# Gathering q during the second expert layer, k during the third and v during the attention, with six result buffers

## The chip, the cores and the metric

The kernel runs on one core of one Trainium2 chip. A core has five engines that each run an instruction stream of their own: PE (matmuls), DVE and ACT (element-wise work, copies out of PSUM), POOL (here mostly index-driven transfers) and SP (here only plain transfers). PEld is PE's loading of weights, shown as an engine of its own. Transfers from any of them are carried out by 16 DMA engines. The metric is the time on the device, in microseconds (us): the median of three runs. Beside the runs stands one profiled execution, from which all views below are taken.

## The reference

For 16 sequences of 256 tokens with 256 features, `x` first goes through a causal cross-attention with 16 heads, whose keys and values come from a context of the same size, and the result is added to `x`. After a layer norm, three "fast feedforward" layers (ffn q, k and v) follow. Each sends a token down a binary tree of depth 4 to one of 16 experts and applies only that expert's two small matrices:

```
leaf   = tree(x, node_w, node_b)                 # one of 16, per token
hidden = relu(x @ w1[leaf] + b1[leaf])           # 256 -> 64
out    = hidden @ w2[leaf] + b2[leaf]            # 64 -> 256
```

With q, k, v from the three layers, the last step is a plain attention within each sequence, over 256 features at once: `x + softmax(q k^T / 16) v`.

## The kernel before

The kernel has three stages. The **first** (lines 154 to 674) computes the cross-attention in groups of two sequences, the layer norm, the routing of every token, and a sort by expert: for each ffn, POOL scatters the normalised rows (`xnb`, 128 rows of 1 KB in a transfer) into DRAM arrays `xs`, so that the tokens of an expert lie together. Some scatters of ffn 1 and 2 are left over and are sent by `send_one` during the second stage.

The **second** (`second_stage`, line 723) runs the experts. For each of the three ffns there are NJ = 47 tiles of 128 sorted tokens, 141 steps in all, written out by hand: the order of PE, DVE and POOL is the order of the program. In step `i`:

- SP fetches the rows of tile i+6 (`fetch`, L758, 128 KB into one of ten `xt` buffers; the address is read from a table in SBUF by a register load, L755).
- DVE copies the expert's first matrix to a fixed place (`staged`, L775, one of four `ws1`), PE turns the tile (`turn`, L784), ACT copies it out.
- PE does the first matmul of tile i-2 (`layer1`, L795), and ACT applies bias and relu into one of four `hT` (L797).
- PE does the second matmul of tile i-3 (`layer2`, L805). For every pair of tiles DVE copies the result into one of three buffers `y` (L811), and SP writes it to the DRAM array `ys` (L813, 256 KB). A buffer can be used again when that write has landed.
- In steps 47, 51 and 55 DVE also works out, for one ffn each, where in `ys` every token's row stands (`spots`, L743 to L747).

To go back to the order of the tokens, POOL gathers 128 rows of `ys` at a time (L857, one transfer of 128 KB). Each of q, k and v needs 32 gathers, and each can start only when all of its `ys` has been written. POOL is kept in step with the rest by a tiny copy, `tick` (L831), that reads the newest `hT` before each of its transfers; `hT` in turn cannot be overwritten before its tick has read it. The line that says in which steps POOL sends something, and the orders in which the generators of `gathers` hand out the transfers, are these:

```python
if i % 2 == 0 and (4 <= i < 40 or f == 1 and j >= 12) or f == 2 and j >= 4 and i % 4 != 3:
```

```python
if f == 1:
    order = [(0, t) for t in range(EARLY)]                                                # EARLY = 16
elif f == 2:
    order = [(g, t) for t in range(ROOM) for g in (1, 0) if g or t >= EARLY]              # ROOM = 24
```

So during ffn 0 the left-over scatters are sent; during ffn 1, 16 gathers of q in every second step; during ffn 2, 24 gathers of k and 8 more of q, in three of four steps. Each goes into a buffer of its own (24 for q, 24 for k).

The **third** stage (`third_stage`, line 863) is the attention, in 32 query tiles. Here only PE's order is written by hand, the other engines' order comes from a scheduler. POOL has to do the remaining 48 gathers: all 32 of v, into six buffers that come free with the results, and the last eight of q and of k, into buffers that come free when PE has turned the first sequences. In the built program POOL's first gathers of the stage are two of q and two of k, then v 0 to 5, then eight more of q and k, and so on. For a query tile PE turns q and k (L879), multiplies them (L887), turns the probabilities (L902) and multiplies them with v (L911); DVE and ACT do the softmax between, and SP writes the tile out (L914).

Of the kernel before, what the change touches and what calls it, by code (L numbers as in the profile page):

```python
# [30 lines left out]
FP = mybir.dt.float32  # L31
# [6 lines left out]
P = 128  # L38
NB, S, D = 16, 256, 256
# [5 lines left out]
NF, NL, NN, HW = 3, 16, 15, 64  # L45
PB = 2
TP = PB * S
NP = NB // PB
# [9 lines left out]
def xattn_ffn(ctx: ExitStack, tc: tile.TileContext, x, ctxT, wq, wk, wv, wo,  # L58
              node_w, node_b, w1, b1, w2, b2, out):
    nc = tc.nc  # L60
    PS = bass.MemoryType.PSUM
    ET = mybir.EngineType
# [6 lines left out]
    ys = [nc.dram_tensor(f"ys_{f}", (NJ * P, D), FP, kind="Internal").ap() for f in range(NF)]  # L69
# [14 lines left out]
    for e in range(2):  # L84
        for dst, n, row in ((own, DH, DH * e), (first, 1, DH * (1 - e))):
            t = const.tile([P, 1], FP, tag=f"rows{e}{n}", name=f"rows{e}{n}")
# [67 lines left out]
    def first_stage(stack):  # L154
# [514 lines left out]
        def finish():  # L669
            send(len(rows))  # L670
            ending[0] = False
            return scatters, lambda: send(1)

        return finish

# [47 lines left out]
    def second_stage(stack, scatters, send_one, rest):  # L723
        one = stack.enter_context(tc.tile_pool(name="f_one", bufs=1, **AFTER))
        three = stack.enter_context(tc.tile_pool(name="f_three", bufs=3, **AFTER))
        ten = stack.enter_context(tc.tile_pool(name="f_ten", bufs=10, **AFTER))
        ps = stack.enter_context(tc.tile_pool(name="ps_f", bufs=2, space=PS, **AFTER))
        leaf_weights(2, one, nc.sync)
# [71 lines left out]
        def layer2(i):  # L800
            f, j = work[i]
            if j % 2 == 0:
                ys_ps[f, j // 2] = ps.tile([P, 2, D], FP, tag="y", name=f"py_{f}_{j}")
            py = ys_ps[f, j // 2]
            nc.tensor.matmul(py[:, j % 2, :], hT[i % NBUF],  # L805
                             w2_sb[f][:, bass.ds(leaf_of.pop(i), 1), :].rearrange("h l d -> h (l d)"),
                             start=True, stop=True)
            if j % 2 or j == NJ - 1:
                n = j % 2 + 1
                y = three.tile([P, 2, D], FP, tag="y", name=f"y_{f}_{j}")  # L810
                nc.vector.tensor_copy(y[:, 0:n], py[:, 0:n])  # L811
                j0 = j - j % 2
                nc.sync.dma_start(out=ys[f][j0 * P:(j + 1) * P, :].rearrange("(t p) d -> p t d", p=P), in_=y[:, 0:n])  # L813

        fetched = {i: fetch(i) for i in range(6)}
        for i in range(len(work) + 4):
            if i + 6 < len(work):
                fetched[i + 6] = fetch(i + 6)
            if i in (NJ, NJ + 4, NJ + 8):
                spots((i - NJ) // 4)  # L820
            if i < len(work):
                staged(i)
                turn(i, fetched.pop(i))
            if 0 <= i - 2 < len(work):
                layer1(i - 2)
            if 0 <= i - 3 < len(work):
                layer2(i - 3)
            f, j = divmod(i, NJ)
            if i % 2 == 0 and (4 <= i < 40 or f == 1 and j >= 12) or f == 2 and j >= 4 and i % 4 != 3:

                nc.gpsimd.tensor_copy(tick, hT[(i - 2) % NBUF][0:1, 0:1])  # L831
                if f == 0:
                    send_one()
                else:
                    next(rest[f], None)
        assert next(rest[1], rest) is rest and next(rest[2], rest) is rest


    ROOM, EARLY = 24, 16

    def gathers(pool, f):


        if f == 1:
            order = [(0, t) for t in range(EARLY)]
        elif f == 2:
            order = [(g, t) for t in range(ROOM) for g in (1, 0) if g or t >= EARLY]
        else:
            order = []
        for b in range(NB if f == NF else 0):  # L850
            order += [(2, 2 * b), (2, 2 * b + 1)]
            if 3 <= b < 3 + (2 * NB - ROOM) // 2:
                t = ROOM + 2 * (b - 3)
                order += [(g, t + i) for g in range(2) for i in range(2)]
        for f, t in order:
            g = pool.tile([P, D], FP, tag=f"g{f}", bufs=6 if f == 2 else ROOM, name=f"g_{f}_{t}")
            nc.gpsimd.indirect_dma_start(  # L857
                out=g, out_offset=None, in_=ys[f],
                in_offset=bass.IndirectOffsetOnAxis(ap=spot_of[0][:, f, t:t + 1], axis=0))
            got[f, t] = g  # L860
            yield

    def third_stage(stack, rest):
        two = stack.enter_context(tc.tile_pool(name="a_two", bufs=2, **AFTER))
        three = stack.enter_context(tc.tile_pool(name="a_three", bufs=3, **AFTER))
        ps = stack.enter_context(tc.tile_pool(name="ps_a", bufs=2, space=PS, **AFTER))

        def wanted(f, t):
            while (f, t) not in got:
                next(rest)  # L870
            return got.pop((f, t))

        def turn(b, f):

            pt = ps.tile([P, DC, S], FP, tag="t", name=f"pt_{f}_{b}")
            for i in range(2):
                g = wanted(f, 2 * b + i)
                for c in range(DC):
                    nc.tensor.transpose(pt[:, c, i * P:(i + 1) * P], g[:, c * P:(c + 1) * P], ident)  # L879
            tT = two.tile([P, DC, S], FP, tag=f"T{f}", name=f"T_{f}_{b}")  # L880
            (nc.scalar.copy if f else nc.vector.tensor_copy)(tT, pt)
            return tT

        def probs(b, qt, qT, kT):
            pz = ps.tile([P, S], FP, tag="z", name=f"pz_{b}_{qt}")
            for d in range(DC):
                nc.tensor.matmul(pz, qT[:, d, qt * P:(qt + 1) * P], kT[:, d, :],  # L887
                                 start=(d == 0), stop=(d == DC - 1))
            mx = three.tile([P, 1], FP, tag="fmx", name=f"fmx_{b}_{qt}")
            nc.vector.tensor_reduce(mx, pz, AX.X, ALU.max)  # L890
            nc.vector.tensor_scalar(mx, mx, -D ** -0.5, None, ALU.mult)
            pr = three.tile([P, S], FP, tag="pr", name=f"pr_{b}_{qt}")
            den = three.tile([P, 1], FP, tag="den", name=f"den_{b}_{qt}")
            nc.scalar.activation(pr, pz, AF.Exp, bias=mx, scale=D ** -0.5, accum_out=den)
            rd = three.tile([P, 1], FP, tag="frd", name=f"frd_{b}_{qt}")
            nc.vector.reciprocal(rd, den)
            return pr, rd

        def turned(b, qt, pr):
            pt = ps.tile([P, 2, P], FP, tag="u", name=f"ptf_{b}_{qt}")  # L900
            for kt in range(2):
                nc.tensor.transpose(pt[:, kt, :], pr[:, kt * P:(kt + 1) * P], ident)  # L902
            pT = two.tile([P, 2, P], FP, tag="fpT", name=f"fpT_{b}_{qt}")
            nc.scalar.copy(pT, pt)
            return pT

        def result(b, qt, pT, rd, v):
            t = 2 * b + qt
            po = ps.tile([P, D], FP, tag="o", name=f"po3_{t}")
            for kt in range(2):  # L910
                nc.tensor.matmul(po, pT[:, kt, :], v[kt], start=(kt == 0), stop=(kt == 1))  # L911
            ot = three.tile([P, D], FP, tag="ot", name=f"ot_{t}")
            nc.vector.scalar_tensor_tensor(ot, po, rd, xres[:, t, :], ALU.mult, ALU.add)
            nc.sync.dma_start(out=out[t * P:(t + 1) * P, :], in_=ot)  # L914

        n = 2 * NB
        made, pTs, turns, vs = {}, {}, {0: (turn(0, 0), turn(0, 1))}, {}
        for i in range(n + 2):
            b, qt = divmod(i, 2)
            if i < n:  # L920
                made[i] = probs(b, qt, *turns[b])
                if b + 1 < NB:
                    turns.setdefault(b + 1, []).append(turn(b + 1, qt))
            if 0 < i <= n:
                pTs[i - 1] = turned(*divmod(i - 1, 2), made[i - 1][0])
            if i > 1:
                b, qt = divmod(i - 2, 2)
                if qt == 0:
                    vs[b] = [wanted(2, 2 * b + kt) for kt in range(2)]
                result(b, qt, pTs.pop(i - 2), made.pop(i - 2)[1], vs[b])  # L930

    spot_of, got = [], {}
    with ExitStack() as stack:
        with tc.manual_schedule(engines={ET.PE, ET.DVE, ET.Activation, ET.Pool}):
            finish = first_stage(stack)
        scatters, send_one = finish()
    pool = ctx.enter_context(tc.tile_pool(name="gather", bufs=2, **AFTER))
    rest = [gathers(pool, f) for f in range(NF + 1)]
    with ExitStack() as stack:
        with tc.manual_schedule(engines={ET.PE, ET.DVE, ET.Pool}):  # L940
            second_stage(stack, scatters, send_one, rest)
    with tc.manual_schedule(engines={ET.PE}):
        third_stage(ctx, rest[NF])


# [33 lines left out]
```

## Time and profile before

| | |
|---|---|
| median of the runs | 721.13 us (721.12 to 721.37) |
| the profiled execution's own time | 746.15 us |
| its span, first to last instruction | 744.2 us |
| mean granted PE clock | 0.929 |
| busy, share of the span: PE, PEld, DVE, ACT, POOL | 83%, 62%, 56%, 48%, 48% |
| first `ph` matmul of the second stage | at 446.5 us |
| first turned q of the third stage | at 640.1 us |
| gathers of `ys` rows (L857) | 96, 963 ns of POOL each |
| stores of `ys` (L813) and loads of `xt` (L758) | 72 and 141 |

The profiled execution is 25 us longer than the runs. Times in the views count from the start of the span. In a list of instructions the columns are start, duration, engine, line, operation, output<-input, count, and in brackets how long the engine was idle before and what ended it; "issue" means that the profile shows nothing it waited for. A wait is put down to the release that came last.

### The profile page before, as it was taken

The page shows a single profiled execution, that of the slowest core. Times are in us where ns is not written, and L with a number is a line of the kernel's source. Part 1 is how long each engine was busy: PE and PEld are TensorE (multiplying, and loading weights), DVE is VectorE, ACT ScalarE, POOL GpSimd, SP SyncE. Part 2 cuts the span into 40 slices and gives each one's busy share as a digit, 9 for nine tenths or more (in the row PEclk, how much of TensorE's full clock was granted, in tenths as well). Part 3 has the DMA queues.
Part 4 walks back from the last instruction along what each step waited for, and adds up shares of the span by engine and source line. Part 5 has one row for each costly group of instructions (what it writes and reads, how often), then busy time and mean ns, then how long its engine had stood idle before and what let it go on. Part 6 is the DMA issues. An engine that isn't in the chain of part 4 may idle for free.

```text
span 744.2 us, 17407 instructions
## 1 busy us (share of the span) xinstructions
PE 619.8 (83%) x5453; PEld 458.7 (62%) x5453; DVE 417.7 (56%) x1924; ACT 353.8 (48%) x920; POOL 357.9 (48%) x530
## 2 busy tenths in 40 slices
PE   4579999999898999989874529998998788847998
PEld 2346666666565655656553318777986667636886
DVE  0157777868677786876864253445543243414564
ACT  5457666665665556455332105543554344313443
POOL 7133554267576566665674413410341565664331
PEclk9779999999999999999987558998999899969999
DMA  9303942002011110111112316876787787433333
GB/s 263 106 17 101 324 129 61 1 24 80 30 59 48 37 61 30 37 51 44 44 43 93 92 43 210 256 229 207 233 261 219 232 258 226 148 104 93 114 114 93
DMA packets 65388, 89.59 MB, mean 120 GB/s; under 512 B 7921, under 2 KB 54289, under 8 KB 65297
## 3 DMA queue, kind: packets, MB, share of 16 engines
q1 hardware_dynamic: 53186, 52.77, 23.2%
q0 software_dynamic: 12112, 35.71, 16.0%
q8 instruction: 45, 0.74, 0.4%
q14 instruction: 45, 0.37, 0.2%
HBM read 46.90 MB, written 41.55 MB: 119 GB/s over the span
## 4 chain that ended last, share of the span: by engine, by line
PE 61%; DVE 11%; POOL 7%; issue 7%; ACT 6%; DMA 5%; SPq 1%; another core or an unknown queue 1%; DVEq 0%; POOLq 0%; ACTq 0%
PE ph L795 8%; PE py L805 7%; PE bank L275 6%; PE bank L452 6%; PE bank L472 6%; PE pz L887 4%; PE po L911 4%; PE px L784 4%; PE bank L427 4%; PE bank L304 3%; DMA ys<-y 3%; PE bank L295 3%; DVE junk L434 2%; PE pt L879 2%; POOL xs L407 2%
## 5 line engine op out<-in xcount | busy, mean ns | idle before, releaser
L434 DVE CUSTOM_DVE_ANT_0 junk<-bank,later 128x128 bf16<-128x128 f32 (+1 forms) x512 | 147.7, 352 | 24.4 <-PE bank L427 22.1
L462 POOL TENSOR_SCALAR_AFFINE_SELECT pT<-pT 128x1024 f32<-128x1024 f32 x64 | 70.3, 1098 | 137.7 <-ACT pT L457 128.9
L457 ACT ACTIVATE pT<-bank 128x384 f32<-128x384 f32 x256 | 104.6, 493 | 67.1 <-PE bank L452 40.8
L857 POOL DMA_INDIRECT g<-ys,spot_i x96 | 92.5, 963 | 72.0 <-PE po L911 31.9
L407 POOL DMA_INDIRECT xs<-xnb,dest_i x96 | 95.9, 999 | 28.4 <-issue 20.1
L795 PE MATMUL ph<-xT,ws 128*128 128x128 f32 x564 | 91.6, 287 | 12.8 <-DVE ws L775 10.0
L811 DVE COPY y<-py 128x512 f32<-128x512 f32 x72 | 48.9, 680 | 85.7 <-DMA ys<-y 29.3
L805 PE MATMUL py<-w,hT 65*128 x282 | 88.8, 397 | 7.8 <-ACT hT L797 5.8
L797 ACT ACTIVATE hT<-ph,b_sb 64x128 f32<-64x128 f32 x141 | 51.1, 362 | 81.9 <-PE ph L795 48.7
L795 PEld LDWEIGHTS ph<-xT,ws 128*128 128x128 f32 x564 | 77.5, 199 | 17.9 <-issue 9.7
L452 PE MATMUL bank<-xqT,xkT 32*128 32x256 f32 (+1 forms) x1024 | 71.5, 356 | 12.4 <-DVE xqT L443 4.4
L452 PEld LDWEIGHTS bank<-xqT,xkT 32*128 32x128 f32 x1024 | 57.7, 192 | 34.2 <-DVE xqT L443 14.9
L472 PE MATMUL bank<-pT,va 128*32 128x256 f32 (+1 forms) x1024 | 57.5, 343 | 17.8 <-DVE mx L434 9.3
L427 PE MATMUL bank<-xkT,xqT 32*128 32x128 f32 (+1 forms) x1024 | 63.9, 361 | 0.0
L784 PE MATMUL px<-ident,xt 128*128 128x128 f32 x282 | 57.0, 284 | 4.8 <-DMA xt<-xs 4.2
L788 ACT COPY xT<-px 128x512 f32<-128x512 f32 (+1 forms) x71 | 41.3, 582 | 39.0 <-PE px L784 34.6
L831 POOL COPY tick<-hT 1x1 f32<-1x1 f32 x67 | 12.0, 179 | 96.1 <-ACT hT L797 95.4
L784 PEld LDWEIGHTS px<-ident,xt 128*128 128x128 f32 x282 | 40.2, 147 | 23.8 <-DMA xt<-xs 5.8
L472 PEld LDWEIGHTS bank<-pT,va 128*32 128x32 f32 x1024 | 29.8, 112 | 37.7 <-issue 19.1
L222 ACT ACTIVATE junkq<-xres,negm 128x256 bf16<-128x256 f32 x64 | 31.8, 502 | 43.4 <-DVE negm L217 33.4
L775 DVE COPY ws<-w 128x128 f32 x141 | 33.7, 240 | 31.0 <-DVE ws L775 14.5
L805 PEld LDWEIGHTS py<-w,hT 65*128 65x128 f32 x282 | 44.5, 198 | 10.0 <-ACT hT L797 7.1
(166 smaller groups left out, 1038.0 us busy)
## 6 DMA issues: line engine op xcount, KB each, us to landing
xt<-xs SPq DMA_DIRECT2D x141, 128.0 KB
ys<-y SPq DMA_DIRECT2D x69, 256.0 KB
xs<-zero POOLq DMA_DIRECT2D x3, 2048.0 KB
xres<-in_x SPq DMA_DIRECT2D x8, 512.0 KB
ctx<-in_ctxT SPq DMA_DIRECT2D x8, 512.0 KB
w<-in_w POOLq DMA_DIRECT2D x4, 1024.0 KB
out<-ot SPq DMA_DIRECT2D x32, 128.0 KB
w<-in_w SPq DMA_DIRECT2D x2, 1024.0 KB
```

The lines of the kernel that those rows point to most:

```text
L407: s = nc.gpsimd.indirect_dma_start(out=xs[f], out_offset=bass.IndirectOffsetOnAxis(ap=dest_i[:, t, f:f + 1], axis=0), in_=row, in_offset=None)
L427: nc.tensor.matmul(bk[g][:, qt * P:(2 * qt + 1) * P], q[r, qt * P:(qt + 1) * P], k[r, 0:(qt + 1) * P], start=True, stop=True)
L434: nc.vector.tensor_tensor_reduce(junk[:, 0:n], bk[g][:, qt * P:qt * P + n], later[:, S - n:], -1.0, -MASKED, ALU.add, ALU.min, mxs[c % 2][ ...
L452: nc.tensor.matmul(bk[g][:, 0:3 * P].rearrange("p (k n) -> p k n", n=P)[:, kt:3 - kt:2 - kt, :], k[r, kt * P:(kt + 1) * P], q[r, kt * P:], ...
L457: nc.scalar.activation(pf[:, g, :], bk[g][:, 0:3 * P], AF.Exp)
L462: nc.gpsimd.affine_select(out=pf[:, :, 0:S], in_=pf[:, :, 0:S], compare_op=ALU.is_ge, fill=0.0, base=0, pattern=[[0, G], [0, 2], [1, P]], ...
L472: nc.tensor.matmul(av[r, kt * P:], vas[p % 2][:, 2 * b + kt, 8 * (c // 2) + 2 * g + c % 2, :], pT[:, g, kt:3 - kt:2 - kt, :], start=(kt == ...
L784: nc.tensor.transpose(pt[:, i % 2, c, :], xt[:, c * P:(c + 1) * P], ident)
L795: nc.tensor.matmul(ph, w[:, c, :], xTs[i // 2][:, i % 2, c, :], start=(c == 0), stop=(c == DC - 1))
L797: nc.scalar.activation(hT[i % NBUF][0:HW], ph[0:HW], AF.Relu, bias=b1_sb[:, f].rearrange("h c e -> h (c e)")[:, bass.ds(leaf(i, ET.Activat ...
L805: nc.tensor.matmul(py[:, j % 2, :], hT[i % NBUF], w2_sb[f][:, bass.ds(leaf_of.pop(i), 1), :].rearrange("h l d -> h (l d)"), start=True, st ...
L857: nc.gpsimd.indirect_dma_start(out=g, out_offset=None, in_=ys[f], in_offset=bass.IndirectOffsetOnAxis(ap=spot_of[0][:, f, t:t + 1], axis=0))
```

## The change

Four things are edited.

1. The gathers of q are all put into ffn 1 and those of k all into ffn 2: 32 each, in the steps with tile number j from 7 on, except where j is a multiple of five. (8 of 40 steps are left out.) The scatters during ffn 0 stay where they were. One generator hands out all 64.
2. For the 32 gathers of one kind there is now less need of buffers of their own, because tiles that are no longer read take the rest: the first-layer weights `w1_sb[0]` (eight places) for q, and `w1_sb[1]` (eight) with the last two normalised tiles `xnb` (four each) for k. q has 24 buffers and k 16.
3. In the third stage POOL gathers only v, in an order that is now written by hand too: two before the first query tile, then one a query tile, two ahead, into six buffers as before.
4. The result buffers `y` are six instead of three.

```diff
@@ first_stage, finish @@
-            return scatters, lambda: send(1)
+            return scatters, lambda: send(1), [xns["b", p] for p in range(NP - 2, NP)]
@@ second_stage @@
+        six = stack.enter_context(tc.tile_pool(name="f_six", bufs=6, **AFTER))
...
-                y = three.tile([P, 2, D], FP, tag="y", name=f"y_{f}_{j}")
+                y = six.tile([P, 2, D], FP, tag="y", name=f"y_{f}_{j}")
...
-            if i % 2 == 0 and (4 <= i < 40 or f == 1 and j >= 12) or f == 2 and j >= 4 and i % 4 != 3:
+            if f == 0 and i % 2 == 0 and 4 <= i < 40 or 0 < f < NF and j >= 7 and j % 5:
                 nc.gpsimd.tensor_copy(tick, hT[(i - 2) % NBUF][0:1, 0:1])
                 if f == 0:
                     send_one()
                 else:
-                    next(rest[f], None)
+                    next(rest, None)
@@ gathers @@
-    def gathers(pool, f):
...
+    def gathers(pool, sent):
+        for f in range(2):
+            old = [w1_sb[f].rearrange("p c (t d) -> p (c t) d", d=D)] + (sent if f else [])
+            old = [t[:, i] for t in old for i in range(t.shape[1])]
+            room = 2 * NB - len(old)
+            for t in range(2 * NB):
+                got[f, t] = gather(pool.tile([P, D], FP, tag=f"g{f}", bufs=room, name=f"g_{f}_{t}") if t < room
+                                   else old[t - room], f, t)
+                yield
+
+    def gather(g, f, t):
+        nc.gpsimd.indirect_dma_start(
+            out=g, out_offset=None, in_=ys[f],
+            in_offset=bass.IndirectOffsetOnAxis(ap=spot_of[0][:, f, t:t + 1], axis=0))
+        return g
@@ third_stage @@
-        def wanted(f, t):
-            while (f, t) not in got:
-                next(rest)
-            return got.pop((f, t))
+        def v(t):
+            if t < n:
+                got[2, t] = gather(pool.tile([P, D], FP, tag="g2", bufs=6, name=f"g_2_{t}"), 2, t)
...
+        for t in range(2):
+            v(t)
...
         for i in range(n + 2):
             b, qt = divmod(i, 2)
+            v(i + 2)
@@ at the end @@
-    with tc.manual_schedule(engines={ET.PE}):
-        third_stage(ctx, rest[NF])
+    with tc.manual_schedule(engines={ET.PE, ET.Pool}):
+        third_stage(ctx, pool)
```

More of the change, by code (lines that the diff above doesn't have):

```diff
@@ L834, in second_stage, with third_stage @@
                 else:
-                    next(rest[f], None)
-        assert next(rest[1], rest) is rest and next(rest[2], rest) is rest
-    ROOM, EARLY = 24, 16
-    def gathers(pool, f):
[L844 to L863, printed above, removed]
+                    next(rest, None)
+        assert next(rest, rest) is rest
+    def gathers(pool, sent):
[12 more added lines that the diff above has]
+        return g
+    def third_stage(stack, pool):
         two = stack.enter_context(tc.tile_pool(name="a_two", bufs=2, **AFTER))
@@ L876, in turn @@
             for i in range(2):
-                g = wanted(f, 2 * b + i)
+                g = got.pop((f, 2 * b + i))
                 for c in range(DC):
@@ L928, in third_stage @@
                 if qt == 0:
-                    vs[b] = [wanted(2, 2 * b + kt) for kt in range(2)]
+                    vs[b] = [got.pop((2, 2 * b + kt)) for kt in range(2)]
                 result(b, qt, pTs.pop(i - 2), made.pop(i - 2)[1], vs[b])
@@ L935, in xattn_ffn @@
             finish = first_stage(stack)
-        scatters, send_one = finish()
+        scatters, send_one, sent = finish()
     pool = ctx.enter_context(tc.tile_pool(name="gather", bufs=2, **AFTER))
-    rest = [gathers(pool, f) for f in range(NF + 1)]
+    rest = gathers(pool, sent)
     with ExitStack() as stack:
```

## The prediction

> **What bounds the kernel now.** I read the shares by engine first (PE busy 83% of 744.2 us, DMA uneven), then the busy time by stretch, which cuts the span into the stages that the edit touches. Columns: stretch, its length, busy us (instructions) of PE, PEld, DVE, ACT, POOL, then granted clock, DMA share, GB/s.
>
> ```profile
> 446.00:503.60 57.60, 54.00 (x358) 46.46 (x358) 22.99 (x63) 28.72 (x68) 19.02 (x34) 0.96 0.75 229
> 503.60:565.80 62.20, 56.49 (x378) 49.56 (x377) 29.70 (x81) 30.16 (x72) 18.75 (x33) 0.95 0.79 233
> 565.80:640.00 74.20, 62.23 (x391) 51.48 (x390) 28.77 (x76) 30.53 (x74) 37.01 (x64) 0.95 0.76 227
> 640.00:681.30 41.30, 23.40 (x113) 18.76 (x111) 11.44 (x36) 8.99 (x28) 25.24 (x27) 0.81 0.39 116
> 681.30:744.20 62.90, 59.32 (x338) 51.95 (x337) 35.30 (x110) 27.00 (x84) 20.20 (x22) 0.99 0.35 103
> ```
>
> The first three rows are the three ffns, q, k and v, 47 tiles each. In PE's timeline a tile takes 1.10 us when nothing is late, so 47 need 51.7 us. The ffns therefore lose 57.6 - 51.7 = 5.9, 62.2 - 51.7 = 10.5 and 74.2 - 51.7 = 22.5 us. The last two rows are the attention stage: from 681.3 on a query tile takes 2.385 us (25 tiles to 740.9, then the tail); in the 41.3 us before only 7 were finished, which at that pace need 16.7. The loss there is 24.6 us, with DMA at 0.39 and PE busy 57%. So 63 us of the span are stalls in exactly these stages. Before 446 us the edit changes nothing but one load (below).
>
> Next, the waits in the three ffns (us in total, times, longest), and the chain of waits at the start of the attention stage (start, us, what).
>
> ```profile
> DVE y L811 <- DMA ys<-y: 29.3, 26, 2.9
> ...
> PE ph L795 <- DVE ws L775: 10.0, 11, 3.0
> ```
>
> ```profile
> 646.97 2.52 DMA g<-ys,spot_i
> ...
> 652.83 11.14 issue
> 663.98 2.08 PE pz L887 x4
> ```
>
> DVE waits 29.3 us for a result buffer `y` whose write has not landed; the expert weights `ws` are copied on the same in-order engine, so PE waits behind. One such delay grows: PE's timeline at the border of ffns 0 and 1 (start, us, engine, line, what, count, idle before it):
>
> ```profile
> 505.97 0.38 PE L784 MATMUL px<-ident,xt 128*128 128x128 f32 x2
> 509.33 1.19 PE L795 MATMUL ph<-xT,ws 128*128 128x128 f32 x4 [2.97 <-DVE ws L775]
> ...
> 515.43 0.47 PE L784 MATMUL px<-ident,xt 128*128 128x128 f32 x2
> 516.62 0.38 PE L784 MATMUL px<-ident,xt 128*128 128x128 f32 x2
> ```
>
> DVE came late to the row positions (1.6 us of `own`, `spot`, `spot_i`), PE stood still, and its matmuls then took twice their time (1.06 against 0.61 us for a group) until 515.4: four tiles in 10.65 us instead of 4.4, 6.25 us for one late DVE. Last, POOL's timeline at ffn 2:
>
> ```profile
> 573.04 0.17 POOL L831 COPY tick<-hT 1x1 f32<-1x1 f32 x1 [7.88 <-ACT hT L797]
> 579.35 0.97 POOL L857 DMA_INDIRECT g<-ys,spot_i  x1 [6.13 <-DMA xt<-xs]
> 580.32 0.21 POOL L831 COPY tick<-hT 1x1 f32<-1x1 f32 x1
> 580.70 0.98 POOL L857 DMA_INDIRECT g<-ys,spot_i  x1 [0.16 <-issue]
> 581.68 0.18 POOL L831 COPY tick<-hT 1x1 f32<-1x1 f32 x1
> 582.02 0.98 POOL L857 DMA_INDIRECT g<-ys,spot_i  x1 [0.16 <-issue]
> ```
>
> The first k gather stood 6.13 us for the last k rows to be written, then six went out back to back, 1.33 us apiece. Just there, at 582 to 589, ACT, DVE and SP all hang (waits of 3.3 and 5.0 us whose releaser is unknown; SP's small instructions each start 0.7 us late), PE takes 12.75 us for five tiles (582.26 to 595.01), 7.3 over its pace, 2.1 of them at half clock. The 11.14 us at 652.8 has the same companion: 16 gathers in a row, 1.25 us apart, while ACT stands from 649.9 to 663.3.
>
> **Part by part.**
>
> Six `y` buffers. A buffer now comes round after six pairs (13.2 us) instead of three (6.6); the chain of waits has steps of 2.4 to 3.8 us on such a write, so I let the 29.3 us of DVE waits go. What PE loses to them, tile by tile over 1.10 us: 5.3 us in ffn 0, about 3 before 565, 3.2 at 567 to 580, and the 6.25 at the border if DVE now arrives early (the last position group, at 518, cost PE nothing). What is late next: SP. It issues two loads and one store per pair; undisturbed 2.31 us, with its hitches about 2.5, so 1.25 us a tile against PE's 1.10, and its lead shrank from 5.7 to 3.2 us between tiles 10 and 26. I give ffn 0 only 3 of its 5.3 us back (ends: 0 and 5.3).
>
> q gathers: 32 instead of 16 in ffn 1, from tile 7 and in four of five tiles, not from 12 in every second. Each issues a tick (0.18), a gather (0.98) and gaps, 1.33 us of POOL; four of them take 5.3 of the 5.5 us of five tiles, so POOL runs nearly back to back. Behind POOL stand only more gathers and ACT: `hT` cannot be overwritten before its tick has read it, four tiles later, which a POOL up to 4.4 us late does not reach. Cost of a gather to PE: 0 by ffn 1 (row below, one every second tile, PE busy 20.83 of 21.0 us at 261 GB/s); 0.41 us by ffn 2 after 593.7 (three of four tiles; 30 tiles in 42.1 us, 9.1 over their pace, beside 22 gathers); 1.2 us by the burst (7.3 us over six). The pattern is nearest to steady ffn 2: 0.41 x 32 = 13.2 us; ends 0 and 39.
>
> ```profile
> 530.00:551.00 21.00, 20.83 (x151) 18.59 (x150) 9.20 (x26) 11.88 (x29) 10.62 (x19) 1.00 0.90 261
> ```
>
> Against ffn 1's present loss of 10.5, which goes with the `y` waits: +2.7.
>
> k gathers: 32 in ffn 2 as before, but from tile 7 instead of 4. The last k store leaves three tiles earlier relative to that, so neither the 6.13 us wait nor the burst should come: -7.3 us; the `y` waits there go (-3.2); 32 gathers cost 13.2 instead of 9.1 over 22 (+4.1). Sum -6.4 (ends -19.6, all gathers free, and +19, all at the burst's price).
>
> One rule of the Trainium skill speaks against this. "DMA: Bandwidth & Descriptors", section "Issuing engines are not separate DMA queues", says that transfers started from SP, ScalarE or GpSimd share the same 16 DMA engines and interleave, so a gather moved from the attention stage (share 0.35 to 0.39) to an ffn (0.75 to 0.79) takes its room from `xt` and `ys`. Per tile ffn 1 would ask 131 + 131 + 0.8 x 131 = 367 KB; in 1.10 us that is 333 GB/s, more than any 10 us of this trace moved (268 at share 0.90, so some 295 when full). By the rule, 16 x 131 KB = 2.1 MB at 265 GB/s lengthen the ffns by 7.9 us. By the row above, 16 gathers cost nothing; by ffn 2's row (245 GB/s, gaps left) something other than bytes decided. I take the 13.2 above, which is more than the rule asks; with the rule's 7.9 in its place the sum below would be 5.3 us lower.
>
> Attention stage: 32 gathers instead of 48, v first and two ahead. The q and k gathers that stood before v (640.7 to 645.7) go, but v's must wait for the last `ys` write, landing near 643.4, and the first result needs two of them: the 2.5 us wait stays. The run of 16 shrinks to six. If the hang goes with the run, 11.1 us, the slow clock after it (2) and a second stop at 676 to 679 (4) go: -16; if the hang has another cause, about 0. Later v gathers wait for a freed buffer as before.
>
> At nothing: gathers into `w1_sb` 0 and 1 and two `xn` tiles, whose last readers end over 20 us before in ffns 0 and 1; ACT's and DVE's order in the attention stage is unchanged in the built kernel. The larger pool moves addresses, so ffn 2's w1 load now waits for the last normalising (about 426 us, was 402); with w2's, 2 MB at 250 GB/s end near 435, ahead of the first `xt` at 441.8. Without that cover it would be up to 8 us.
>
> **Sum.** -3 + 2.7 - 6.4 - 16 = -22.7 us of the profiled 746.15. The runs shown have a median of 721.13, 25 us less: part of what the profiled execution loses is not there, and hangs of sequencers are the likeliest part. So I count the two hang terms at half (8 of 16, and 3.65 of 7.3): -3 + 2.7 - 2.75 - 8 = -11, giving 710 us.
>
> **Rivals.** (a) Slower: back-to-back gathers hang the sequencers wherever they stand, now through ffn 1 too. With p us lost per gather the change is 64p + 3 (ffn 0's rest) - 38.9 (what the ffns lose now) - 12 (attention, between its ends), zero at p = 0.75. The burst's 1.2 speaks for it, the 0.41 of steady ffn 2 and 0 in ffn 1 against. At p = 1 it is +16: 737 us. (b) SP and the 16 engines set the ffns: the `y` wait becomes a wait for `xt`, the ffns gain 3 and pay 7.9, attention gains 8: 718 us. For it: SP's 1.25 us a tile, the rule; against: 1.10 us a tile for 20 us at share 0.90. (c) The hang is no matter of gathers and stays: only the ffn terms, -3: 718 us.
>
> **How the numbers follow.** Forecast (700 to 715) 0.5; (c) 0.12; (b) 0.14; (a) 0.2; a better end, both hang terms whole and gathers free, 0.04. Range 694 to 727: (a)'s upper part is left out. A difference of 0.2%, 1.4 us, is about what a measurement can tell from no change. Faster 0.71 (the forecast, the better end, most of (b) and (c)), same 0.06, slower 0.23 ((a), and the edges of (b) and (c)).
>
> **What would show it.** No `DVE y <- DMA ys<-y` in the waits; no half-clock tiles near 510; ffn 1 between 58 and 66 us and ffn 2 near 65; no POOL gather waiting 6 us at ffn 2; no stop over 5 us in the first ten query tiles. Wrong if ffn 1 passes 75 us with SP, ACT and DVE hanging beside POOL, or if PE comes to wait for `xt`.

## The result, and the profile after

The changed kernel takes 712.58 us (four runs, 708.78 to 714.19) against 721.25 us of the kernel before (721.12 to 722.24): a ratio of 0.9869, 95% interval 0.9829 to 0.9909, or 8.7 us less. The forecast was 710, the range 694 to 727.

One thing has to be known before the profiles are compared. The median of the kernel before is 721 to 724 us in four groups of runs made for this case, but 745.8 us in another group on another chip, where all seven runs lie between 744.57 and 747.37. Whether that is the chip or its condition on that day, no run tells. The profiled execution that the prediction read, of 746.15 us, is of the second kind by its time and by its stages (ffn 2 74.2 us and attention 104.2; 74.2 and 102.9 in experiment 10 on that chip); the times beside it are of the first kind, and so is the profile after. The comparison below is therefore with another profile of the kernel before, on a chip of the first kind (experiment 1: 723.29 us, span 721.3). I call the two kinds the 722 us chips and the 746 us chip. One slow execution each of experiment 5 (3091.63 us) and experiment 8 (1003.03 us) is left out of their times.

The stages, from the first turned tile (`px`) of each ffn and the first turned q (`pt`) of the attention stage in PE's timeline:

| us | before, 722 us chip | after | difference | forecast, hang terms halved |
|---|---|---|---|---|
| until ffn 0 | 443.3 | 440.6 | -2.7 | 0 |
| ffn 0 | 60.8 | 58.4 | -2.4 | -3 |
| ffn 1 | 59.0 | 66.1 | +7.1 | +2.7 |
| ffn 2 | 66.1 | 64.7 | -1.4 | -2.75 |
| attention | 92.1 | 82.5 | -9.6 | -8 |
| sum | 721.3 | 712.3 | -9.0 | -11 |

The busy time by stretch (columns as in the prediction: stretch, length, busy us of PE, PEld, DVE, ACT, POOL, clock, DMA share, GB/s), first of the kernel before on the 722 us chip, ffn 1, ffn 2 and the first part of the attention stage:

```profile
504.10:563.10 59.00, 53.36 (x377) 47.12 (x376) 29.27 (x78) 30.01 (x72) 18.84 (x33) 1.00 0.79 236
563.10:629.20 66.10, 58.19 (x392) 48.89 (x391) 29.23 (x76) 31.36 (x74) 37.16 (x64) 1.00 0.85 258
629.20:672.50 43.30, 35.42 (x192) 29.36 (x191) 19.72 (x62) 14.71 (x46) 30.36 (x32) 0.96 0.48 142
```

and of the changed kernel:

```profile
499.00:565.10 66.10, 57.23 (x377) 46.91 (x376) 30.64 (x80) 30.20 (x72) 36.19 (x62) 0.97 0.83 250
565.10:629.80 64.70, 59.70 (x392) 51.21 (x391) 28.12 (x73) 31.03 (x74) 38.22 (x66) 0.95 0.87 269
629.80:650.00 20.20, 18.92 (x111) 16.04 (x110) 11.19 (x35) 8.63 (x26) 9.47 (x10) 1.00 0.41 125
```

In ffn 1 POOL's instructions go from 33 to 62 and the length from 59.0 to 66.1 us, at a DMA share of 0.83. In the attention stage PE is busy 35.4 of the first 43.3 us before, and 18.9 of 20.2 after. Single executions of one kernel differ by 5 us among these four (708.8 to 714.2) and by 8 us in the largest group (717.8 to 726.2, kernel before), and the profiled one is the longest of its four, so a term of 2 us in the table is no more than an indication.

The waits in the ffns (us in total, times, longest), of the kernel before on the 722 us chip, 443 to 630 us:

```profile
DVE y L811 <- DMA ys<-y: 43.4, 31, 2.8
...
PE px L784 <- DMA xt<-xs: 4.1, 2, 3.8
```

and of the changed kernel, 440 to 630 us:

```profile
DVE y L812 <- PE py L806: 69.3, 58, 4.5
...
PEld px L785 <- DMA xt<-xs: 27.9, 27, 4.1
...
PE px L785 <- DMA xt<-xs: 16.3, 12, 3.8
```

The line `DVE y L811 <- DMA ys<-y` is gone: DVE now waits for PE. But PE waits for its rows, 16.3 us for `px` where it was 4.1, and that is what the prediction named as a sign that it is wrong.

The attention stage in the chain of waits, before (722 us chip):

```profile
652.74 0.90 issue
653.64 2.75 DMA g<-ys,spot_i
...
661.17 2.72 DMA g<-ys,spot_i
663.93 0.90 PE po L911 x2
```

PE stands for v 7, sent at 653.64 us with 12 gathers of q and k ahead of it in the stage, and for v 9, sent at 661.17 with 16 ahead: POOL sends 30 gathers without a break from 629.8 to 667, 1.25 us apart. After, the chain holds one gather in the stage, v 1, and the write that it follows:

```profile
630.41 2.06 DMA ys<-y
...
634.75 2.81 DMA g<-ys,spot_i
```

From there on a query tile takes 2.385 us up to the last pair, with no stop. The first 2.7 us of the table come from the first stage, in the same chain, before and after:

```profile
402.76 4.56 DMA xs<-xnb,dest_i
```

```profile
402.13 2.44 DMA xs<-xnb,dest_i
```

A scatter on the path lands in 2.44 instead of 4.56 us. Before, SP issues the 1 MB load of ffn 2's first weights at 401.4 us, right beside it; after, at 422.1, because the buffer's address has moved. The kernels here with that load at 422 to 424 us begin ffn 0 at 440.3 to 441.7 (experiment 7 aside, which waits for less); those with it at 401 to 402, at 443.3 to 444.0.

### The profile page after: what moved, and what is told of

Same layout as the page of the kernel before. It is cut to its first block, busy times and chain, and to the rows that moved or that the text cites. A ratio compares the mean times of both kernels' runs of the same rounds, so it can differ in the third digit from the quotient of the medians.

```text
span 712.3 us, 17418 instructions
## 1 busy us (share of the span) xinstructions
PE 614.1 (86%) x5453; PEld 454.2 (64%) x5453; DVE 418.8 (59%) x1924; ACT 354.1 (50%) x920; POOL 361.5 (51%) x545
## 4 chain that ended last, share of the span: by engine, by line
PE 61%; DVE 11%; DMA 8%; POOL 8%; ACT 6%; issue 4%; SPq 1%; DVEq 0%; ACTq 0%; POOLq 0%
PE bank L275 7%; PE ph L796 7%; PE py L806 7%; DMA xt<-xs 7%; PE bank L452 6%; PE bank L472 6%; PE bank L427 4%; PE px L785 4%; PE bank L304 4%; PE po L905 4%; PE pz L881 4%; PE bank L295 2%; DVE junk L434 2%; POOL xs L407 2%; POOL pT L462 2%
## 5 line engine op out<-in xcount | busy, mean ns | idle before, releaser
L853 POOL DMA_INDIRECT g<-ys,spot_i x72 | 69.5, 965 | 59.6 <-PE po L905 30.7
L785 PE MATMUL px<-ident,xt 128*128 128x128 f32 x282 | 58.2, 289 | 18.7 <-DMA xt<-xs 16.3
L785 PEld LDWEIGHTS px<-ident,xt 128*128 128x128 f32 x282 | 38.5, 147 | 42.6 <-DMA xt<-xs 27.9
L472 PEld LDWEIGHTS bank<-pT,va 128*32 128x32 f32 x1024 | 30.1, 112 | 38.4 <-issue 20.2
L832 POOL COPY tick<-hT 1x1 f32<-1x1 f32 x82 | 14.9, 182 | 69.4 <-ACT hT L798 68.5
L443 DVE TENSOR_TENSOR xqT<-bank,xqT 128x256 f32<-128x256 f32 x64 | 26.9, 420 | 37.2 <-PE bank L441 37.2
```

The costliest lines, as they stand in the source:

```text
L472: nc.tensor.matmul(av[r, kt * P:], vas[p % 2][:, 2 * b + kt, 8 * (c // 2) + 2 * g + c % 2, :], pT[:, g, kt:3 - kt:2 - kt, :], start=(kt == ...
L785: nc.tensor.transpose(pt[:, i % 2, c, :], xt[:, c * P:(c + 1) * P], ident)
L853: nc.gpsimd.indirect_dma_start(out=g, out_offset=None, in_=ys[f], in_offset=bass.IndirectOffsetOnAxis(ap=spot_of[0][:, f, t:t + 1], axis=0))
```

## The experiments

All edits are against the kernel before or the changed one, as named. The ratios are to the kernel before on the same chip; times from different groups are best compared by them.

**1. The kernel before, profiled again**

> The kernel before once more, for a second profile of it. Theory 1: the profiled execution of before lost about 25 us in stops of ACT, DVE and SP (582 to 589, 650 to 663) that its ordinary runs do not have. Then this one shows a span near 720 us, ffn 2 near 65 us instead of 74 and the attention stage near 90 instead of 104. Theory 2: the stops belong to the kernel in every run, and the profiled execution is long for another reason: the attention stage is again over 100 us, and the shorter span comes out of the first stage or ffn 0 and 1.

723.29 us. The hangs of the profile on record are not there: beside the same run of gathers ACT and DVE wait for PE or for each other, 5.2 us at most. ffn 1 loses 59.0 - 51.7 = 7.3 us, not 10.5. So on such a chip there was no 11 us hang to win in the attention stage; what it loses there, 9.6 us against after, goes with the queue in front of v (1.6 us up to the first result, the rest in the stops for v 7 and v 9 and after them).

**2. Six result buffers alone** (kernel before; q 16 to 23 are gathered into `w1_sb[0]` to make room)

```diff
-                y = three.tile([P, 2, D], FP, tag="y", name=f"y_{f}_{j}")
+                y = six.tile([P, 2, D], FP, tag="y", name=f"y_{f}_{j}")
```

> One part alone: six result buffers in the kernel before, its gathers where they were (eight of the q gathers land in the first-layer weights of ffn 0, to make room). Theory 1: the wait for a free y buffer turns into a wait for xt, because SP issues two loads and a store in about 2.5 us per pair of tiles and is late anyway: 718 to 721 us, and PE waits for xt in the ffns. Theory 2: the buffers are what the change gains by: 712 to 715 us.

718.38 us, ratio 0.9938 (0.992 to 0.9956): 4.5 us less, some 2 of them the earlier start (441.5). The `y` waits are gone, and PE's wait for `xt` has taken their place (12.8 us for `px`, 28.7 for its weight loads). The buffers move the wait; they remove little.

**3. The changed kernel with three result buffers**

```diff
-                y = six.tile([P, 2, D], FP, tag="y", name=f"y_{f}_{j}")
+                y = three.tile([P, 2, D], FP, tag="y", name=f"y_{f}_{j}")
```

> The other part alone: the changed kernel with three result buffers. Theory 1: the gain lies in the attention stage, and the denser gathers in ffn 1 cost more with three buffers than with six (the y waits come back on top): 713 to 719 us, attention stage still near 83 us. Theory 2: the buffers are what the change gains by: 720 us or more, with DVE waits for y over 25 us.

714.72 us, ratio 0.9882 (0.9847 to 0.9917), against 0.9869 with six: beside the other edits the buffers are worth 0.9 us, which these intervals cannot tell from nothing. DVE waits 47.1 us for `ys` again, and ffn 1 takes 65.0 us as against 66.1. Whatever bounds the ffns lies behind both waits.

**4. The `ys` writes issued by ACT instead of SP** (changed kernel)

```diff
-                nc.sync.dma_start(out=ys[f]...
+                nc.scalar.dma_start(out=ys[f]...
```

> The changed kernel with the ys stores issued by ACT instead of SP. Theory 1: SP's issuing is what sets the ffns after the change (1.25 to 1.41 us a tile against PE's 1.10); without 72 stores of some 0.5 us it is faster than PE, the waits for xt go, ffn 1 and 2 shrink from 65 to 55 to 60 us each, unless ACT loses what SP gains: 697 to 706 us. Theory 2: the 16 DMA engines are full: the same bytes take the same time, 710 to 714 us.

727.3 us, ratio 1.0062 (1.0044 to 1.0081). The waits for `xt` leave the top of the list, so SP was relieved, but ACT's queue now stands until DVE has made the copy before each write (from 541.54 to 542.54 us, for one); PE waits for `hT` in its place (18.9 us, 46 times), and the ffns take 68, 67 and 68 us. It mixes the relief with a new wait and so decides nothing about SP.

**5 and 6. POOL's order by hand in the attention stage**, on the kernel before and on experiment 2

```diff
-    with tc.manual_schedule(engines={ET.PE}):
+    with tc.manual_schedule(engines={ET.PE, ET.Pool}):
```

> One word of the change alone: in the kernel before, POOL's order in the attention stage is the order of the program, so v 0 to 7 come ahead of the sixteen q and k gathers and each later pair of v ahead of four of those. All gathers stay in the stages where they were, 48 in the attention stage. Theory 1 (v stands in line behind q and k in POOL's queue): the attention stage shrinks from 92 to 84 to 87 us, the time to 715 to 718 us. Theory 2 (it is the number of gathers in the stage, or the load on the DMA engines, that costs): no difference, 720 to 724 us.

> The same with six result buffers: the two parts of the change that take a wait away, without the sixteen gathers moved into ffn 1. Theory 1: the gains add, 4.6 and 5 to 7, and nothing is paid in ffn 1: ffn 1 near 60 us, attention 84 to 87 us, 709 to 713 us, as good as the changed kernel or better. Theory 2 (moving the gathers is what gains): 716 to 719 us.

720.54 us, ratio 0.9961 (0.9937 to 0.9985), and 715.96 us, 0.9912 (0.9884 to 0.994): both miss what was expected of the order (715 to 718 and 709 to 713). With v in front, the first results come as early as in the changed kernel, but 48 gathers remain, and this order puts four of q and k to each of the pairs 3 to 6. Six gathers of 1.25 us are 7.5 us where a pair of query tiles takes 2 x 2.385 = 4.77: the stop now comes at query tiles 12 to 15, and the stage takes 87.4 and 89.2 us instead of 92.1, not 82.5. The order alone brings 4.7 of the stage's 9.6 us on the kernel before, and 1.3 on experiment 2 (whose stage took 90.5 us).

**7. Addresses of `xt` fixed** (changed kernel; it leaves out the reading of the addresses, so it fetches other rows than the sorted tokens; bytes and transfers are the same)

```diff
-            at = nc.values_load(row[0:1, NF + f, j:j + 1], engines=[ET.SP], ...
-            ld = nc.sync.dma_start(out=xt, in_=xs[f][bass.ds(at, P), :])
+            ld = nc.sync.dma_start(out=xt, in_=xs[f][j % NL * (P + T):j % NL * (P + T) + P, :])
```

> The changed kernel with xt fetched from fixed addresses: SP does not read the table (some 0.35 to 0.41 us and 0.15 us of register work per tile go); the fetched rows are zeros of the right size instead of the sorted tokens, the same bytes. Theory 1 (SP's issuing sets ffn 1 and 2): 15 to 25 us less, ffns near 55 us each, no waits for xt. Theory 2 (the DMA engines set them): the ffns stay at 58, 66 and 65 us, 709 to 714 us.

687.47 us, ratio 0.9533 (0.9482 to 0.9585), 25 us below the changed kernel. ffn 1 in the busy time by stretch:

```profile
488.40:542.40 54.00, 53.07 (x377) 46.43 (x376) 32.10 (x80) 29.72 (x72) 36.27 (x62) 1.00 0.95 298
```

PE is busy throughout, and with 31 gathers ffn 1 is 1 us longer than ffn 0 with none (53.0), at 298 GB/s and a share of 0.95. So neither the gathers nor their bytes cost PE more than about 1 us as long as the rows arrive. This edit takes away the table read and makes the address a constant, both at once; experiment 12 takes away reads alone. ffn 0 also begins 5.2 us earlier (435.4 us), and none of its loads needs the table any more.

**8. Half the bytes of `xt`** (changed kernel; half of each row is fetched and used twice, half of the features are left out)

```diff
-            ld = nc.sync.dma_start(out=xt, in_=xs[f][bass.ds(at, P), :])
+            ld = nc.sync.dma_start(out=xt[:, 0:P], in_=xs[f][bass.ds(at, P), 0:P])
```

> The changed kernel with half of each xt row fetched (512 bytes instead of 1 KB) and used twice: the same number of instructions on every engine and of rows, 64 KB less for each of 141 tiles; half of the features are left out. Theory 1 (SP's issuing sets the ffns): same as the changed kernel, 709 to 714 us. Theory 2 (the bytes on the DMA engines set them): ffn 1 and 2 shrink by 5 us or more each, 698 to 704 us.

707.63 us, ratio 0.9801 (0.9735 to 0.9866): 5 us for a fifth to a quarter of the ffns' bytes, just under the one expectation and well above the other. ffn 1 takes 60.4 us instead of 66.1, ffn 2 65.9 instead of 64.7. Bytes therefore have a part in it, but PE still waits 14.5 us for `xt`, and SP's own table reads get shorter with the bytes (385 ns on average in ffn 1 instead of 419), so the run does not part the two theories. SP's instruction list shows no gap over 60 ns on average between its instructions; it issues one tile in 1.21 us in ffn 0 and 1.29 in ffn 1 (1.29 x 47 = 60.6, about the length of ffn 1). It is never idle and never ahead. In the changed kernel itself, SP's timeline in ffn 1 (one issue, or two with the read between them, and their time) reads

```profile
551.50 1.27 SPq L759 DMA_DIRECT2D xt<-xs  x2
552.87 0.38 SPq L814 DMA_DIRECT2D ys<-y  x1
553.80 1.58 SPq L759 DMA_DIRECT2D xt<-xs  x2
```

The other spaces hold table reads, too. From 500 to 560 us, 43 tiles in 60 us, one tile costs SP: table read 0.47 us with its gap, issue of the `xt` transfer 0.37, address and semaphore work 0.22, and half a `ys` write 0.33, together 1.39, against PE's 1.10. In ffn 0, without gathers, the sum is 1.24: the table read takes 0.39. From there to ffn 1 it is the table reads (349 to 419 ns on average) and the share of the writes that grow. The gathers' part shows in ffn 1 alone: the mean read is 348, 360, 358 and 359 ns with 16 gathers (experiments 1, 2, 5 and 6), and 419 and 417 ns with 31 (the changed kernel and experiment 3). The median stays at 277 to 278 ns in ffns 0 and 1 of the changed kernel: single reads, of up to 1.04 us, make the difference. Over 47 tiles 0.06 us are 3 us.

**9 and 10. One table read for four tiles**, on the changed kernel and on experiment 2

```diff
-            at = nc.values_load(row[0:1, NF + f, j:j + 1], engines=[ET.SP], ...
+            if j % 4 == 0:
+                m = min(j + 4, NJ)
+                _, places = nc.values_load_multi_w_load_instructions(row[0:1, NF + f, j:m], engines=[ET.SP], ...
+                at_of.update(((f, j + k), p) for k, p in enumerate(places))
+            at = at_of.pop((f, j))
```

> The changed kernel; only SP's table reads differ: one register load fetches the row positions of four tiles at a time (36 loads instead of 141), the transfers and their order are the same. In the run with half rows SP stood without any gap over 40 ns at 1.21 us a tile in ffn 0 and 1.29 in ffn 1, against PE's 1.10, and a table read with its gap is 0.40 to 0.45 us of that. Theory 1 (SP's issuing bounds the expert stages, and the moved gathers cost by slowing it): SP falls to about 0.9 us a tile, PE's 1.10 becomes the bound, the three ffns take 53 to 57 us each, as with fixed addresses, and the time falls by 17 to 25 us to 688 to 696 us. Theory 2 (it is the reads of addresses known only at run time, scattered over memory, or the 16 DMA engines, that are slow): no more than 5 us, 708 to 714 us, and PE still waits for xt.

> The kernel before with six result buffers and with SP's table reads four at a time; gathers as before (16 in ffn 1, 32 in ffn 2, 48 in the attention stage). Theory 1: the ffns go to 53 to 56 us each here too, and the attention stage keeps its loss of 5 to 8 us, so the time is 693 to 704 us. Against the same edit on the changed kernel it is then 5 to 10 us slower, the whole price of the 16 late gathers, since 16 gathers moved into ffn 1 would cost nothing once SP is ahead; with the table reads one by one that difference was 5.8 us, of which ffn 1 had taken back about 6. Theory 2: 713 to 718 us, 4 to 6 us above the same edit on the changed kernel.

These two, and number 11, fell on the 746 us chip. 723.38 us, ratio 0.9698 (0.9669 to 0.9727), and 727.27 us, 0.9754 (0.9697 to 0.9812). Both miss both expectations. The waits of PE for `xt` are gone from the top of the list in both. ffn 1 with 31 gathers in four of five steps (first row, experiment 9) and with 16 in every second step (second row, experiment 10):

```profile
495.50:564.10 68.60, 58.52 (x377) 50.60 (x376) 30.87 (x80) 29.82 (x72) 36.20 (x62) 0.95 0.81 246
```

```profile
493.60:547.60 54.00, 53.14 (x377) 46.18 (x376) 30.33 (x80) 29.63 (x72) 18.90 (x33) 1.00 0.88 268
```

Half of the expectation holds: where gathers are sparse or absent (ffn 0 of the two, 54.2 and 52.7 us, and ffn 1 of experiment 10) PE runs at its pace. The other half doesn't: on this chip 15 more gathers cost 68.6 - 54.0 = 14.6 us, 0.97 us each, though SP has time to spare. ffn 2, with 32 gathers in three of four or four of five steps, takes 73.8 and 74.2 us. ACT and DVE stand still together for 0.8 to 2.7 us at a time, six times in ffn 1 and eleven times in ffn 2 of experiment 9, while POOL goes on issuing (ACT from 594.3 to 597.2 us, DVE from 594.5 to 598.6; SP issues nothing from 596.4 to 600.0). In experiment 7, with gathers as dense on a 722 us chip, that happens not once. It looks like the hang of the profile on record, and it comes back in the attention stage of experiment 10, where 48 gathers are left:

```profile
639.99 0.95 POOL L866 DMA_INDIRECT g<-ys,spot_i  x1 [0.30 <-issue]
641.24 0.95 POOL L866 DMA_INDIRECT g<-ys,spot_i  x1 [0.30 <-issue]
...
645.18 0.58 ACT L890 COPY T<-pt 128x512 f32<-128x512 f32 x1 [12.64 <-remote]
```

ACT stands 12.64 us with nothing in the profile that it waits for ("remote" is a release that the profile doesn't show), in a run of gathers without a break from 622.5 to 642. The stage takes 102.9 us there and 83.6 in experiment 9, which has v's gathers alone.

**11. `xt` fetched nine tiles ahead instead of six** (changed kernel)

```diff
-            if i + 6 < len(work):
-                fetched[i + 6] = fetch(i + 6)
+            if i + 9 < len(work):
+                fetched[i + 9] = fetch(i + 9)
```

> The changed kernel with the rows of a tile fetched nine tiles ahead instead of six (ten buffers as before), all else the same. If PE waits for xt because single fetches land late (3.5 us from issue to landing, a few longer), three more tiles of lead hide that: the ffns lose 10 to 20 us less, 693 to 703 us. If SP issues fewer tiles a microsecond than PE uses up (1.24 to 1.41 us a tile against 1.10), the lead is used up after some 15 to 25 tiles and nothing is refilled: at most 3 x 1.1 = 3 us, 709 to 713 us, and the waits for xt stay.

729.95 us, ratio 0.9808 (0.9761 to 0.9855), on the 746 us chip, on which the changed kernel itself has no run; so its time settles nothing. Its ffn 1 and 2 (74.4 and 71.9 us) are full of the stops of that chip. On the same chip ffn 0 takes 56.3 us with the longer lead and 54.2 with fewer table reads.

**12. Fewer table reads, and the gathers spread** (experiment 9, with 20 q gathers in every second step of ffn 1, 27 of k in two of three steps of ffn 2, and the other 17 in the attention stage, each behind the v gather of its query tile, in three of four tiles)

```diff
-            if f == 0 and i % 2 == 0 and 4 <= i < 40 or 0 < f < NF and j >= 7 and j % 5:
+            if f == 0 and i % 2 == 0 and 4 <= i < 40 or f == 1 and j >= 7 and j % 2 or f == 2 and j >= 7 and j % 3:
...
             v(i + 2)
+            if i % 4 != 3:
+                next(rest, None)
```

> The changed kernel with the table reads four at a time, and with its gathers less dense: 20 of q in ffn 1, in every second step (which on the last chip cost PE nothing: ffn 1 54.1 us with 16, against 68.6 with 31 in four of five steps), 27 of k in ffn 2, in two of three steps, and the 17 that are left in the attention stage, each behind the v gather of its query tile, in three of four tiles. If SP's issuing is what bounds the ffns and dense gathers are what stops the sequencers, then on a chip where the kernel before takes about 722 us: ffns 0 and 1 at 53 to 55 us, ffn 2 at 54 to 58, attention 82 to 86, in all 684 to 694 us, a ratio of 0.947 to 0.961. On a chip like the last, where it takes 746: ffns 0 and 1 the same, ffn 2 between 58 and 70, attention 83 to 90, in all 692 to 710 us, 0.928 to 0.952. If the fixed addresses of the earlier run helped by something else than the missing table reads, then at 722 us of before: 700 to 712 us. If it is the number of gathers in a stage that costs, not their spacing, ffn 1 loses 8 us or more here, and the attention stage too.

690.52 us against 723.73, ratio 0.9545 (0.9518 to 0.9571), on a 722 us chip: it beats both kernels (the changed one has 0.9869). The numbers of the first theory were met. ffn 0, which has no gathers and so differs from the changed kernel by the table reads alone, went from the first of these rows to the second:

```profile
440.60:499.00 58.40, 55.78 (x363) 48.63 (x364) 24.41 (x64) 28.72 (x68) 18.96 (x34) 0.91 0.72 225
```

```profile
440.50:494.00 53.50, 53.30 (x362) 46.18 (x363) 24.25 (x64) 29.08 (x68) 19.03 (x34) 0.96 0.86 269
```

That is 4.9 us for the reads, with the address still one known only at run time. It is beyond the scatter of single profiles: with one read a tile ffn 0 takes 56.3 to 60.8 us in all of them (experiments 4 and 7 aside), with one read for four tiles 52.7 to 54.2 us in all three. ffn 2 takes 56.5 us; ffn 1 and the attention stage:

```profile
494.00:548.80 54.80, 53.60 (x378) 46.44 (x377) 30.48 (x80) 29.79 (x72) 22.73 (x40) 1.00 0.88 267
...
605.30:688.20 82.90, 77.75 (x449) 67.75 (x447) 46.61 (x146) 36.11 (x112) 46.42 (x49) 1.00 0.47 136
```

The last row settles experiments 5 and 6 as well: 49 gathers in the attention stage cost nothing (82.9 us; 82.5 with the 32 of the changed kernel) when v goes first and the others come at 1.5 to a pair of query tiles: 3.5 x 1.25 = 4.4 us of POOL, under the pair's 4.77.

## Why the prediction was right in its number, and where its steps were not

The sign and the size were right (-8.7 us for -11), in part by luck. In the profiles ffn 1 cost 4.4 us more than forecast; 2.7 us in the first stage, which the sum had at nothing, and 1.6 us more in the attention stage made up for most of it, and the attention term was right in size for another cause than the one given. Of the signs that were named, the `y` wait, the half-clock tiles near 510 us and the long stops in the attention stage are gone, but PE came to wait for `xt`, which was to show that the prediction is wrong: in that step it was.

- **Six buffers, ffn 0 given back 3 us.** -2.4. Right, and so was "what is late next: SP". The step failed in how far it went: I let SP take back a part of ffn 0 alone. SP's issuing bounds all three ffns of the changed kernel. By times, the buffers alone bring 4.5 us with the earlier start, and beside the other edits 0.9.
- **Cost of a gather in ffn 1, 0.41 us; net +2.7.** +7.1. This is the term that was mis-sized. The price was about right: with 31 gathers ffn 1 takes 66.1 and 65.0 us (changed kernel, experiment 3), with 16 it takes 59.0, 60.5, 62.9 and 64.2 (before and experiments 2, 5, 6), so 15 more cost 3.9 us between the means and 7.1 in the pair of profiles, 0.26 to 0.47 us each. What failed is the loss they were set against: "ffn 1's present loss of 10.5, which goes with the `y` waits". On the chips of the runs that loss was 7.3 us, the 6.25 us at the border of the ffns were 2.2, and the rest didn't go with the buffers, since SP stood behind them. The mechanism of the price was another one, too: SP is behind PE already in ffn 0 (1.24 us a tile against 1.10), and beside 31 gathers its table reads are longer by 0.06 us than beside 16, some 3 of the 4 to 7 us; where the rest goes is not traced. With fixed addresses 31 gathers cost 1 us (experiment 7), with fewer reads 20 sparser ones cost 1.3 (experiment 12, ffn 1 against ffn 0).
- **The rule of the Trainium skill.** "DMA: Bandwidth & Descriptors", section "Issuing engines are not separate DMA queues", has all transfers share the 16 DMA engines; by it the prediction estimated that the 16 moved gathers lengthen the ffns by 7.9 us. ffn 1 did grow by 7.1, but not for that reason: experiment 7 moved the same bytes at 298 GB/s in 54.0 us. The section's next sentence says that starting transfers from several engines saves only the sequencer's time to initiate one, "which is usually small relative to the DMA itself". Here that time, 1.24 to 1.39 us a tile with the read of the address, was the bound, and experiment 12, which takes up to 0.3 us of it away and spreads the gathers, is some 22 us faster.
- **k gathers, -7.3 for the wait and the burst.** The wait did shrink, from 6.13 us (6.44 on the 722 us chip) to the 4.29 of this row of POOL's timeline, and seven went out back to back all the same:

```profile
579.13 0.98 POOL L853 DMA_INDIRECT g<-ys,spot_i  x1 [4.29 <-DMA xt<-xs]
```

  So "neither the 6.13 us wait nor the burst should come" failed for the burst. On this chip it hangs neither SP nor ACT and DVE, but in the midst of it PE waits 2.67 us for `xt` (until 588.94), and its groups of matmuls then take 1.06 us instead of 0.61 up to 594.5. ffn 2 gained 1.4 where the halved sum had 2.75.
- **Attention, -16, halved to -8.** -9.6, right in size for a reason that I hadn't given. The hang that the term was made of is not there on a 722 us chip. What is there is v behind up to 16 other gathers. I had named that queue, but counted only the hang beside it. On the 746 us chip, hang and queue together, the whole term was a good one: 102.9 against 83.6 us, 19.3, between experiments 10 and 9.
- **Halving the hang terms** because the runs were 25 us under the profile was the right doubt; that the two came from chips with different times could not be seen from one profile.
- **At nothing: the load of ffn 2's weights.** Its new place goes with a gain of 2.1 us on the path, in a scatter beside the place that it left. I had asked only whether it would be late at the place that it goes to.
- **The rivals.** (b) was right in its mechanism: the `y` wait became a wait for `xt`, and the ffns together lost 3.3 us, for which it had 4.9. Its sum of 718 us missed the 2.7 us of the first stage and 1.6 us each in the ffns and the attention stage. (a) is real, but only on the 746 us chip and, there, at p = 0.97 by ffn 1 of experiments 9 and 10; even so the kernel with the dense gathers was 4 us faster there, since the attention stage gave back 19.3, where (a) had 12. (c) is out: the attention stage gained.

Not settled: what stops ACT, DVE and SP beside dense gathers on the one chip and not on others; the changed kernel's own time on that chip; and how much of experiment 12's gain over the changed kernel belongs to each of its two edits on a 722 us chip, where experiment 9 has no run; ffn 0's 4.9 us are the reads' alone.

## What to carry to other kernels

When a wait for a buffer is removed, add up the instructions of the queue that feeds it: an issuing engine with no gaps between its instructions may be the bound, though the page counts it as idle, and a run with fixed addresses tests it. Count a gather stream by its rate against the consumer (here 1.25 us of POOL each, 4.77 us a pair), and let what is needed first stand first in the queue. And when a profile is longer than the runs shown, profile once more before any term is built on its stalls.

## What the runs showed of the hardware that was not expected

- One chip needs 745.8 us for the program that others run in 721 to 724. The difference lies beside dense indirect transfers of GpSimd: with the fewer table reads an ffn with one of them in every second step or less takes 52.7 to 54.2 us there, 53.5 to 54.8 elsewhere, but one with them in three of four or four of five steps takes 68.6 to 74.2 there, and ACT stands up to 12.64 us.
- A register load of one table value on SP takes 261 ns at best and 0.39 us on average in the changed kernel; of four values 295 ns at best and 0.54 us on average (experiment 12). At best, three more values take 34 ns more.
- The 16 DMA engines moved 298 GB/s over 54 us, at a share of 0.95, with PE busy 98% beside it.
